# One 32-batch tanh recurrence between the two feed-forward passes of a first layer, in place of two 16-batch recurrences interleaved with them

## The chip, the core and the metric

The kernel runs on one NeuronCore of a Trainium2 chip. The core has a matrix engine (TensorE, "PE" in the profile, with its weight loads as "PEld"), a vector engine (VectorE, "DVE"), an activation engine (ScalarE, "ACT"), a general engine (GpSimd, "POOL") and a queue engine (SyncE, "SP") that issues DMAs. Each works through its own list of instructions in order and waits on semaphores for the others.

The metric is the device time of one execution in microseconds (us), the median of several runs.

## What is computed

The model has two layers. The first one is, with x of shape (32 batches, 256 times, 128 features):

```
x = x + mamba(layernorm(x))        # both directions
x = x + ffn(layernorm(x))          # feed-forward with 8 experts
x = x + recurrence(layernorm(x))   # the change is here
x = x + ffn(layernorm(x))          # the same feed-forward again
```

The recurrence is a plain tanh network over time:

```
def recurrence(x, A, B, C, gamma, beta):
    xb = einsum('bsd,ed->sbe', x, B)
    def step(h, xb_t):
        h = tanh(h @ A.T + xb_t)
        return h, h @ C.T
    _, ys = scan(step, zeros(batch, d), xb)     # 256 steps
    out = transpose(ys, (1, 0, 2)) + x
    return layernorm(out) * gamma + beta
```

A step needs the state of the step before it, so the 256 steps of a batch can only follow each other; batches are independent. A second layer (two attentions and two feed-forwards with routed experts) comes behind and is not touched.

## The kernel before

All activations stay in on-chip memory as 16 chunks `xs[c]` of 128 features by 512 columns, a chunk being two batches of 256 times. The first layer after the mamba part is `first_layer` (L894). It runs two passes over the 16 chunks:

- `before(c)`: the feed-forward `l0_ffn` (L693), then `enter`, which normalises the chunk and writes it into `xin`, the input of the recurrence.
- `behind(c)`: `leave`, which multiplies the states with C (`rnnC`, L856), adds `xin`, normalises (L863) and adds to `xs[c]`; then `l0_ffn` again.

`l0_ffn` is a generator of 23 pieces: norm (L326 to L330, with `spread`, L311 to L320), a short convolution (L715), the router (L724 to L764), eight experts (L770 to L781, a product, a SiLU, four transposed broadcasts of the weights, a multiplication), an output product (L785), a second norm, a down projection with GELU (L796, L798) and an up projection whose sum into `x` (L803) is the last thing a chunk does. Each call also has SP issue two of 60 DMAs that fill a table in HBM with zeros (L673). `enter` and `leave` add 4 and 5 pieces.

`pipeline` (L336) weaves the chunks: a new one starts every five rounds, and in each round every active chunk emits its next piece. So some five to six chunks are in work at a time. What this order gives is what each engine runs; a scheduler in the framework may still swap neighbouring instructions that do not depend on each other.

The recurrence is held by `Recurrence` (L818), here in two groups of 16 batches (chunks 0 to 7 and 8 to 15). `chain` (L831) emits one step per call. For every 32 steps a product with B (`rnnB`, L837, 512 columns that lie 1 KB apart in `xin`) fills one bank of PSUM; each step then adds the product of A with the last state to its 16 columns of that bank (`rnnA`, L846) and takes tanh into `hs` (L849). In the profile an L846 or L837 product in fp32 is two matmuls and two weight loads.

`Beside` (L867) places the steps: each piece that a pipeline emits earns one step, which the active groups take in turn. Chain 0 begins when chunks 0 to 7 have entered, chain 1 when 8 to 15 have. After the first pipeline L920 runs chain 0 to its end, and as long as both are active their steps alternate; the rest of chain 1 goes beside the second pipeline, until chunk 8 leaves, which first runs chain 1 to its end (L915).

The first layer's PSUM has eight banks: six for the tag `m`, one for each chain.

Of the kernel before, what the change touches and what calls it, by code (L numbers as in the profile page):

```python
# [13 lines left out]
F32 = mybir.dt.float32  # L14
# [8 lines left out]
P = 128  # L23
B, L = 32, 256
NT = B * L
CH = 512
NCH = NT // CH
# [247 lines left out]
def hybrid_kernel(ctx: ExitStack, tc, x_d, out_d, d, packs):  # L275
# [18 lines left out]
    def W(name):  # L294
        return com.view(late_t["com"], name) if name in com.at else att.view(late_t["att"], name)
# [7 lines left out]
    def two(ap):  # L303
        return ap.rearrange("p (b t) -> p b t", b=2)
# [18 lines left out]
    def norm(pool, ps, src, bufs):  # L323

        cps = ps.tile([P, CH], F32, tag="m", name="cps")
        nc.tensor.matmul(cps, K("center"), src, start=True, stop=True)  # L326
        sq = pool.tile([P, CH], F32, tag="ln_sq", name="sq", bufs=bufs)
        nc.scalar.activation(sq, cps, AF.Square)
        xc = pool.tile([P, CH], F32, tag="ln_xc", name="xc", bufs=bufs)
        nc.scalar.copy(xc, cps)  # L330
        yield
        rb = yield from spread(pool, ps, sq, 1e-5)
        return xc, rb


    def pipeline(make, every, count=NCH, beside=None, newest=False):  # L336

        active, c, n = [], 0, 0
        while c < count or active:
            if c < count and n % every == 0:  # L340
                active.append(make(c))
                c += 1
            n += 1
            for g in active[::-1] if newest else list(active):
                if next(g, "end") == "end":
                    active.remove(g)
                if beside:
                    beside()

# [1 line left out]
    with ExitStack() as ph:  # L353
# [8 lines left out]
        with tc.tile_pool(name="mtap", bufs=1) as tp, tc.tile_pool(name="mprep", bufs=2, space=PSUM) as pp:  # L362
            tap_t = tp.tile([P, tap.n], F32, name="tap_t")
            nc.scalar.dma_start(tap_t, d["tap"].partition_broadcast(P))
            for k, s in enumerate("fb"):

                wconv[s] = wp.tile([P, DCONV, DI], F32, name="wconv" + s)
                at, _, w = tap.at[s]
# [20 lines left out]
        p2 = ph.enter_context(tc.tile_pool(name="m2", bufs=2))  # L389
        ps = ph.enter_context(tc.tile_pool(name="mps", bufs=2, space=PSUM))  # L390
# [23 lines left out]
        def unit(k):  # L414
# [225 lines left out]
            if s == "b":  # L640
# [4 lines left out]
                yield  # L645

        pipeline(unit, 16, 2 * NCH)

    late = ctx.enter_context(tc.tile_pool(name="late", bufs=1))
# [15 lines left out]
    n = SPARE // 30  # L665
# [141 lines left out]
    def padded(pool, n):  # L807
        out = [pool.tile([P, 2, L + 2], F32, name=f"xp{k}") for k in range(n)]
        for t in out:
            nc.gpsimd.memset(t[:, :, 0:2], 0.0)  # L810
        return out

    NG = 2
    GB, GC = B // NG, NCH // NG

    class Recurrence:  # L818
        def __init__(self, pool, g):
            self.g = g  # L820
            self.xin = pool.tile([P, GB, L], F32, name=f"xin{g}")
            self.hs = pool.tile([P, L, GB], F32, name=f"hs{g}")

        def enter(self, c, pool, ps):

            at = 2 * (c % GC)
            xc, rb = yield from norm(pool, ps, xs[c], 2)
            nc.vector.tensor_mul(self.xin[:, at : at + 2, :], two(xc), two(rb))
            yield

        def chain(self, ps):  # L831
            n = CH // GB
            for t in range(L):
                j = t % n
                if j == 0:
                    hps = ps.tile([P, n, GB], F32, tag=f"h{self.g}", name="hps", bufs=1)
                    nc.tensor.matmul(  # L837
                        hps,
                        W("rnnB"),
                        self.xin[:, :, t : t + n].rearrange("p b t -> p t b"),  # L840
                        start=True,
                        stop=False,
                        skip_group_check=True,
                    )
                if t:
                    nc.tensor.matmul(  # L846
                        hps[:, j, :], W("rnnA"), self.hs[:, t - 1, :], start=False, stop=True, skip_group_check=True
                    )
                nc.scalar.activation(self.hs[:, t, :], hps[:, j, :], AF.Tanh)  # L849
                yield  # L850

        def leave(self, c, pool, ps):

            at = 2 * (c % GC)
            yps = ps.tile([P, CH], F32, tag="m", name="yps")
            nc.tensor.matmul(  # L856
                yps, W("rnnC"), self.hs[:, :, at : at + 2].rearrange("p t b -> p b t"), start=True, stop=True
            )
            o = pool.tile([P, CH], F32, tag="ro", name="o", bufs=2)
            nc.vector.tensor_add(two(o), two(yps), self.xin[:, at : at + 2, :])  # L860
            yield
            xc, rb = yield from norm(pool, ps, o, 2)
            nc.vector.scalar_tensor_tensor(o, xc, W("rnn_g"), rb, ALU.mult, ALU.mult)  # L863
            nc.vector.scalar_tensor_tensor(xs[c], o, W("rnn_b"), xs[c], ALU.add, ALU.add)
            yield

    class Beside:  # L867


        def __init__(self, rate):  # L870
            self.rate, self.due, self.chains = rate, 0.0, []

        def begin(self, chain):
            self.chains.append(chain)

        def step(self):
            chain = self.chains.pop(0)
            if next(chain, "end") != "end":
                self.chains.append(chain)
                return True  # L880
            return False

        def __call__(self):
            self.due = min(self.due + self.rate, 2.0)
            while self.chains and self.due >= 1.0:
                self.due -= 1.0
                self.step()

        def end(self, chain):

            while chain in self.chains:
                self.step()

    def first_layer():  # L894
        with ExitStack() as ph:
            p1 = ph.enter_context(tc.tile_pool(name="l1", bufs=1))
            p2 = ph.enter_context(tc.tile_pool(name="l2", bufs=2))
            ps = ph.enter_context(tc.tile_pool(name="lps", bufs=6, space=PSUM))
            pads = padded(p1, 4)
            groups = [Recurrence(p1, g) for g in range(NG)]  # L900
            beside = Beside(1.0)
            chains = [g.chain(ps) for g in groups]
            done = set()

            def before(c):
                g = c // GC
                yield from l0_ffn(c, p2, ps, pads)
                yield from groups[g].enter(c, p2, ps)
                done.add(c)
                if done >= set(range(g * GC, (g + 1) * GC)):  # L910
                    beside.begin(chains[g])

            def behind(c):
                if c == GC:
                    beside.end(chains[1])  # L915
                yield from groups[c // GC].leave(c, p2, ps)
                yield from l0_ffn(c, p2, ps, pads)

            pipeline(before, 5, NCH, beside)
            beside.end(chains[0])  # L920
            pipeline(behind, 5, NCH, beside)

# [696 lines left out]
    def l1_attn_b(fetch, send):  # L1621
        with ExitStack() as ph:
# [45 lines left out]
            pipeline(chunk, 16, newest=True)  # L1668

    first_layer()  # L1670
    early.close()
    send0, blocks0, fetch0 = l1_ffn(0)
# [5 lines left out]
    with tc.tile_pool(name="last", bufs=4) as p, tc.tile_pool(name="lastps", bufs=2, space=PSUM) as ps:  # L1678

        def leave(c):  # L1680
            yield from fetch1(c, p, ps, 3)
            nc.sync.dma_start(out_d[:, c * CH : (c + 1) * CH], xs[c])

        pipeline(leave, 1)
# [31 lines left out]
```

## Time and profile before

| | us |
|---|---|
| median of 3 runs | 6238.78 (6236.38 to 6243.42) |
| profiled execution | 6234.39 |
| its span | 6232.7 |
| mamba part ends (L644, last) | 2059.3 |
| first norm product of `first_layer` (L326) | 2068.3 |
| first rnnB product (L837) | 2321.6 |
| last xin written (L828, starts) | 2493.95 |
| first rnnC product (L856) | 2640.5 |
| last tanh (L849, starts) | 2857.4 |
| last feed-forward ends (L803, starts) | 3118.7 |

The whole span by engine, and in 40 equal slices of 155.8 us:

```profile
PE 5356.8 (86%) x25850; PEld 2792.6 (45%) x25922; DVE 4117.2 (66%) x7006; ACT 2710.2 (43%) x4424; POOL 3289.4 (53%) x3074
...
PE   6777777777777799999998888897998999997997
PEld 2222222222221466965544444445884444443886
DVE  5998999989989554044555555655665666665565
...
PEclk9888988888988899598989999998998999998998
```

In the first row stands the busy time of each engine, its share of the span and its number of instructions. In the others each digit is one slice: the busy share in tenths, or, in the row PEclk, the clock that TensorE was granted, in tenths of full speed. The first layer after the mamba part covers the slices 14 to 20. The 17th slice (2493 to 2649 us) stands out: PE busy, weight loads at nine tenths, DVE at zero and the clock at five tenths. The recurrence as a whole, in both chains:

```profile
L846 PE MATMUL hps<-hs,com_t x1020: 178/374/396, 2326.3 to 2857.0; 128*128 128x16 f32 x170
L849 ACT ACTIVATE hs<-hps x512: 157/184/203, 2323.6 to 2857.4; 128x16 f32<-128x16 f32 x171
...
L837 PE MATMUL hps<-xin,com_t x32: 1021/1043/1224, 2321.6 to 2828.8; 128*128 128x512 f32 x32
```

The three numbers behind the colon are the shortest, median and longest time of one instruction in ns, then come the first and last start in us. 510 products with A (of two matmuls each), 512 tanh and 16 products with B lie between 2321 and 2858 us.

### The profile page before, as it was taken

The page shows a single profiled execution, that of the slowest core. Times are in us where ns is not written, and L with a number is a line of the kernel's source. Part 1 is how long each engine was busy: PE and PEld are TensorE (multiplying, and loading weights), DVE is VectorE, ACT ScalarE, POOL GpSimd, SP SyncE. Part 2 cuts the span into 40 slices and gives each one's busy share as a digit, 9 for nine tenths or more (in the row PEclk, how much of TensorE's full clock was granted, in tenths as well). Part 3 has the DMA queues.
Part 4 walks back from the last instruction along what each step waited for, and adds up shares of the span by engine and source line. Part 5 has one row for each costly group of instructions (what it writes and reads, how often), then busy time and mean ns, then how long its engine had stood idle before and what let it go on. Part 6 is the DMA issues. An engine that isn't in the chain of part 4 may idle for free. (4 is left out here: it accounts for less than half of the span.)

```text
span 6232.7 us, 73938 instructions
## 1 busy us (share of the span) xinstructions
PE 5356.8 (86%) x25850; PEld 2792.6 (45%) x25922; DVE 4117.2 (66%) x7006; ACT 2710.2 (43%) x4424; POOL 3289.4 (53%) x3074
## 2 busy tenths in 40 slices
PE   6777777777777799999998888897998999997997
PEld 2222222222221466965544444445884444443886
DVE  5998999989989554044555555655665666665565
ACT  4665666666655354344434444342221333333221
POOL 5888888888888564044634444443332333333332
PEclk9888988888988899598989999998998999998998
DMA  3333333333332740000000000004550000000555
GB/s 148 123 123 116 123 116 123 116 123 116 126 112 109 304 185 1 1 1 1 1 1 10 9 8 8 11 8 129 186 172 19 20 16 18 18 11 12 188 188 189
DMA packets 190421, 512.13 MB, mean 82 GB/s; under 512 B 22177, under 2 KB 75169, under 8 KB 164961
## 3 DMA queue, kind: packets, MB, share of 16 engines
q1 hardware_dynamic: 172192, 468.00, 21.1%
q0 software_dynamic: 17280, 35.69, 1.7%
q8 instruction: 205, 3.36, 0.2%
q10 hardware_dynamic: 576, 3.71, 0.2%
q14 instruction: 168, 1.37, 0.1%
HBM read 359.93 MB, written 147.38 MB: 81 GB/s over the span
## 5 line engine op out<-in xcount | busy, mean ns | idle before, releaser
L612 POOL TENSOR_TENSOR dBu<-widedu,bcB 128x512 f32<-128x512 f32 x1024 | 1294.8, 1284 | 249.9 <-DVE h L621 162.0
L621 DVE TENSOR_TENSOR_SCAN h<-dA,dBu 128x512 f32<-128x512 f32 x768 | 942.5, 1227 | 119.8 <-ACT dA L608 30.4
L574 PE MATMUL yps<-pr,cst_t 128*32 128x512 f32 x2048 | 579.9, 645 | 244.8 <-POOL pr L569 102.7
L936 POOL TENSOR_SCALAR_AFFINE_SELECT e<-e 128x2048 f32<-128x2048 f32 (+1 forms) x256 | 343.3, 1353 | 597.2 <-ACT e L1047 386.1
L1412 POOL DMA_INDIRECT rows_out<-y,goes x284 | 271.8, 957 | 559.9 <-DVE y L1410 464.2
L1000 DVE TENSOR_REDUCE nm<-st 128x2 f32<-128x512 f32 x512 | 324.3, 684 | 268.5 <-PE st L996 267.4
L608 ACT ACTIVATE dA<-widedelta,Af 128x510 f32<-128x510 f32 x512 | 348.5, 688 | 300.9 <-DVE h L621 222.0
L608 ACT ACTIVATE dA<-widedelta,Ab 128x510 f32<-128x510 f32 x512 | 345.0, 686 | 272.7 <-DVE h L621 209.5
L1187 ACT ACTIVATE s<-s 128x512 f32<-128x512 f32 x284 | 179.0, 630 | 578.3 <-DVE s L1186 309.2
L574 PEld LDWEIGHTS yps<-pr,cst_t 128*32 128x32 f32 x2048 | 86.8, 112 | 704.8 <-POOL pr L569 228.0
L315 POOL TENSOR_TENSOR rstd<-var,cst_t 128x4 f32<-128x4 f32 x128 | 130.0, 1016 | 516.2 <-DVE var L313 514.4
L781 POOL TENSOR_TENSOR comb<-comb,ye 128x512 f32<-128x512 f32 x224 | 284.8, 1275 | 182.0 <-DVE ye L780 75.2
L1060 ACT ACTIVATE e<-st 128x512 f32<-128x512 f32 x512 | 272.0, 598 | 184.5 <-PE st L1056 154.8
L569 POOL TENSOR_TENSOR pr<-hs,bcC 128x512 f32<-128x512 f32 x256 | 334.4, 1306 | 13.7 <-DVE hs L621 13.7
L621 DVE TENSOR_TENSOR_SCAN hs<-dA,dBu 128x512 f32<-128x512 f32 x256 | 308.3, 1204 | 48.8 <-ACT dA L608 47.3
L1301 POOL DMA_INDIRECT rows_in<-xt,slot x256 | 253.6, 991 | 119.0 <-issue 98.7
L623 DVE TENSOR_TENSOR pr<-h,bcC 128x1024 f32<-128x1024 f32 x256 | 309.8, 1210 | 8.5 <-PE yps L574 0.5
L1188 DVE TENSOR_TENSOR hh<-s,u_ps 128x512 f32<-128x512 f32 x284 | 195.4, 688 | 172.0 <-ACT s L1187 168.0
L1393 PE MATMUL g_ps<-xb,gu 128*128 128x256 f32 x1136 | 302.6, 389 | 3.6 <-ACT xb L1376 2.3
L1402 PE MATMUL yps<-dn,hh 128*128 128x128 f32 x2272 | 291.5, 276 | 5.9 <-DVE hh L1188 5.8
L1393 PE MATMUL u_ps<-xb,gu 128*128 128x256 f32 x1136 | 293.3, 381 | 0.0
L1402 PEld LDWEIGHTS yps<-dn,hh 128*128 128x128 f32 x2272 | 282.8, 192 | 15.3 <-DVE hh L1188 7.8
(353 smaller groups left out, 11248.5 us busy)
## 6 DMA issues: line engine op xcount, KB each, us to landing
gu<-in_gu SPq DMA_DIRECT2D x142, 512.0 KB, 3.7
rows_in<-zero SPq DMA_DIRECT2D x60, 1170.0 KB, 18.7
widedelta<-delta_d SPq DMA_DIRECT2D x64, 1024.0 KB, 5.5
widedu<-du_d SPq DMA_DIRECT2D x64, 1024.0 KB, 5.1
dn<-in_dn SPq DMA_DIRECT2D x142, 256.0 KB, 3.9
bcB<-xdbl_d SPq DMA_DIRECT2D x32, 1024.0 KB, 5.0
bcC<-xdbl_d SPq DMA_DIRECT2D x32, 1024.0 KB, 6.9
xr<-rows_in SPq DMA_DIRECT2D x142, 130.0 KB, 3.8
```

What stands on the lines that cost most here:

```text
L569: nc.gpsimd.tensor_mul(pr, hs, bc["C"][:, g, :])
L574: nc.tensor.matmul(yps[32 * k : 32 * k + 32, :], K("states"), pr, start=False, stop=(g == 3), skip_group_check=True, tile_position=(0, 32 ...
L608: nc.scalar.activation(two(dA)[:, :, 1:L], two(steps)[:, :, 1:L], AF.Exp, scale=A[s][:, at : at + 1])
L612: nc.gpsimd.tensor_mul(dBu, duw[:, k, :], bc["B"][:, g, :])
L621: scan[0] = nc.vector.tensor_tensor_scan(*views, 0.0, ALU.mult, ALU.add)
L623: nc.vector.tensor_mul(pr2, h2, bc["C"][:, g, :].unsqueeze(1).to_broadcast([P, 2, CH]))
L781: nc.gpsimd.tensor_add(comb, comb, ye)
L936: nc.gpsimd.affine_select(e, e, [[0, n], [sign, P]], ALU.is_gt, 0.0, base=base, channel_multiplier=-sign)
L1000: nc.vector.tensor_reduce(n1[:, x, 2 * r : 2 * r + 2], o.rearrange("p (j k) -> p j k", j=2), AX.X, ALU.max, negate=True,)
L1060: nc.scalar.activation(e0[:, r], o.rearrange("p (j k) -> p j k", j=2), AF.Exp)
L1393: nc.tensor.matmul(o[:, j, :], gu[:, at : at + P], xb, start=True, stop=True)
L1402: nc.tensor.matmul(yps[:, t, :], hh[:, k, t * P : (t + 1) * P], dn[:, k, :], start=(k == 0), stop=(k == FF // P - 1),)
```

## The change

One chain carries all 32 batches. `xin` and `hs` are one tile each, a step works on 32 columns, a bank of PSUM holds 16 steps instead of 32, and the chain has two banks under one tag. `Beside` is gone, and with it the call in `pipeline`: the first pipeline runs to its end, then all 256 steps are emitted, then the second pipeline.

```diff
-    def pipeline(make, every, count=NCH, beside=None, newest=False):
+    def pipeline(make, every, count=NCH, newest=False):
...
                 if next(g, "end") == "end":
                     active.remove(g)
-                if beside:
-                    beside()
...
-    NG = 2
-    GB, GC = B // NG, NCH // NG
     class Recurrence:
-        def __init__(self, pool, g):
-            self.g = g
-            self.xin = pool.tile([P, GB, L], F32, name=f"xin{g}")
-            self.hs = pool.tile([P, L, GB], F32, name=f"hs{g}")
+        def __init__(self, pool):
+            self.xin = pool.tile([P, B, L], F32, name="xin")
+            self.hs = pool.tile([P, L, B], F32, name="hs")
         def enter(self, c, pool, ps):
-            at = 2 * (c % GC)
+            at = 2 * c
...
         def chain(self, ps):
-            n = CH // GB
+            n = CH // B
             for t in range(L):
                 j = t % n
                 if j == 0:
-                    hps = ps.tile([P, n, GB], F32, tag=f"h{self.g}", name="hps", bufs=1)
+                    hps = ps.tile([P, n, B], F32, tag="h", name="hps", bufs=2)
...
         def leave(self, c, pool, ps):
-            at = 2 * (c % GC)
+            at = 2 * c
...
-    class Beside:
...
             pads = padded(p1, 4)
-            groups = [Recurrence(p1, g) for g in range(NG)]
-            beside = Beside(1.0)
-            chains = [g.chain(ps) for g in groups]
-            done = set()
+            recurrence = Recurrence(p1)
             def before(c):
-                g = c // GC
                 yield from l0_ffn(c, p2, ps, pads)
-                yield from groups[g].enter(c, p2, ps)
-                done.add(c)
-                if done >= set(range(g * GC, (g + 1) * GC)):
-                    beside.begin(chains[g])
+                yield from recurrence.enter(c, p2, ps)
             def behind(c):
-                if c == GC:
-                    beside.end(chains[1])
-                yield from groups[c // GC].leave(c, p2, ps)
+                yield from recurrence.leave(c, p2, ps)
                 yield from l0_ffn(c, p2, ps, pads)
-            pipeline(before, 5, NCH, beside)
-            beside.end(chains[0])
-            pipeline(behind, 5, NCH, beside)
+            pipeline(before, 5)
+            for _ in recurrence.chain(ps):
+                pass
+            pipeline(behind, 5)
```

More of the change, by code (lines that the diff above doesn't have):

```diff
@@ L865, in leave @@
             yield
-    class Beside:
[L870 to L892, printed above, removed]
     def first_layer():
```

## The prediction

> **What bounds the kernel now.** The page's chain of waits holds only the last 6% of the span, so it says nothing of this change, which lies between about 2060 and 3120 us. I read that stage by windows: first the busy time of every engine, then the tanh row alone, then the instructions in order of time at the few places that price a step.
>
> Busy time by stretch (stretch, its length, busy us and instructions of each engine, granted TensorE clock, DMA share, GB/s):
>
> ```profile
> core 0: us, PE busy (x) PEld busy (x) DVE busy (x) ACT busy (x) POOL busy (x), PEclk, DMA share, GB/s
> 2100.00:2320.00 220.00, 219.08 (x1039) 132.03 (x1039) 133.15 (x337) 114.70 (x172) 139.57 (x117) 1.00 0.72 277
> ...
> 2496.00:2640.00 144.00, 143.97 (x604) 134.11 (x603) 0.00 (x0) 53.94 (x294) 0.00 (x0) 0.50 0.00 1
> ...
> 2830.00:2857.00 27.00, 18.54 (x63) 15.22 (x62) 0.00 (x0) 5.70 (x31) 0.00 (x0) 0.50 0.00 1
> 2866.00:3038.00 172.00, 172.00 (x771) 97.36 (x772) 100.49 (x248) 85.41 (x127) 102.96 (x84) 1.00 0.00 1
> ```
>
> The two feed-forward pipelines keep PE full at clock 1.00. Two stretches hold nothing but the chain: 144 us with both chains and 27 us with one, both at clock 0.50. The tanh row, cut where the stage changes:
>
> ```profile
> 2320.00:2494.60 174.60, 18.76 (x105) 0.93 0.00 1
> 2494.60:2640.50 145.90, 54.46 (x296) 0.50 0.00 1
> 2640.50:2746.30 105.80, 5.18 (x28) 0.84 0.00 1
> 2746.30:2827.70 81.40, 9.16 (x51) 0.98 0.00 1
> 2827.70:2858.00 30.30, 5.89 (x32) 0.50 0.00 1
> ```
>
> Of 512 steps, 184 (105 + 28 + 51) run beside feed-forwards, 328 in the open, 296 of those in pairs. The end of each feed-forward (L803), one per chunk, gives the pace:
>
> ```profile
> 2141.05 0.75 DVE L803 SCALAR_TENSOR_TENSOR x<-m,com_t,x 128x512 f32<-128x512 f32 x1 [0.96 <-PE m L802]
> 2300.16 0.75 DVE L803 SCALAR_TENSOR_TENSOR x<-m,com_t,x 128x512 f32<-128x512 f32 x1 [0.96 <-PE m L802]
> ...
> 2746.29 0.75 DVE L803 SCALAR_TENSOR_TENSOR x<-m,com_t,x 128x512 f32<-128x512 f32 x1 [2.05 <-PE m L802]
> 2866.10 0.75 DVE L803 SCALAR_TENSOR_TENSOR x<-m,com_t,x 128x512 f32<-128x512 f32 x1 [1.92 <-PE m L802]
> 3037.93 0.75 DVE L803 SCALAR_TENSOR_TENSOR x<-m,com_t,x 128x512 f32<-128x512 f32 x1 [1.92 <-PE m L802]
> 3118.70 0.75 DVE L803 SCALAR_TENSOR_TENSOR x<-m,com_t,x 128x512 f32<-128x512 f32 x1 [4.97 <-PE m L802]
> ```
>
> Chunks 0 to 7 without a chain: (2300.16 - 2141.05) / 7 = 22.73 us each. Second pipeline, chunks 3 to 10, no chain left: (3037.93 - 2866.10) / 7 = 24.55 us; its last five chunks drain in 80.8 us.
>
> Last, one chain alone in order of time (start, us, engine, line), at half and at full clock:
>
> ```profile
> 2838.03 0.18 ACT L849 ACTIVATE hs<-hps 128x16 f32<-128x16 f32 x1 [0.70 <-PE hps L846]
> 2838.27 0.50 PEld L846 LDWEIGHTS hps<-hs,com_t 128*128 128x128 f32 x2 [0.38 <-ACT hs L849]
> 2838.27 0.61 PE L846 MATMUL hps<-hs,com_t 128*128 128x16 f32 x2 [0.27 <-ACT hs L849]
> 2838.91 0.18 ACT L849 ACTIVATE hs<-hps 128x16 f32<-128x16 f32 x1 [0.70 <-PE hps L846]
> ...
> 2485.18 0.18 ACT L849 ACTIVATE hs<-hps 128x16 f32<-128x16 f32 x1 [0.48 <-PE hps L846]
> 2485.84 0.18 ACT L849 ACTIVATE hs<-hps 128x16 f32<-128x16 f32 x1 [0.48 <-PE hps L846]
> ```
>
> A lone step is 0.88 us at clock 0.50 (2838.91 - 2838.03) and 0.66 at full clock. Two chains that alternate also need 0.88 us a pair (42 tanh in 20 us, less the rnnB products), since each keeps PE busy while the other is in tanh.
>
> **The change, part by part.** In the built order of the changed kernel all 256 tanh stand together on ACT, with PE's chain between the last product of the first pipeline and the first rnnC product. On PE, POOL and SP everything else stands in the old order, with the same counts; on DVE some small routing operations swap places. So three stretches change.
>
> *First pipeline, without 105 steps beside it.* Chunk 11 ends at 2141.05 + 11 x 22.73 = 2391.1. For the drain I take the second pipeline's, 80.8, less five times the difference of the paces (24.55 - 22.73): 71.7. The last xin (L828) is then written at 2462.8; before it was at 2493.95. **Saved: 31 us**, 0.30 per step moved. In the saturated part a step cost about 0.21 (pace 26.1 with 16 steps against 22.73); 0.21 for all would make 22 us, the low end.
>
> *The chain, alone.* 255 rnnA products replace 510, each on 32 columns. No row has 32 columns, so bound the step. Below: 0.88, if width is free; nothing can make it less at this clock, as weight load, product and tanh wait for each other. PE: a 128x512 product takes 1.03 us a pass at half clock (first norm of the stage, L326: 2.07 for two), 2.0 ns a column, so 16 more columns add 0.032 us a pass; the first pass can lie beside the second weight load (0.29 + 0.22 us), the second can't. ACT: 0.18 us for 16 columns against 0.60 for 512 (L328) is 0.8 ns a column: 0.013. I take 0.88 + 0.032 + 0.013 = 0.925; with both passes and a hand-over somewhat slower, 1.0 at the top. 255 x 0.925 = 236 us.
>
> The rnnB products are still 16, of 512 strided columns, 1.04 us a pass (L837), 2.08 each, the same at either clock. The second bank changes little: in the built order two stand ahead of step 1 (4.2 us), the other 14 each behind the first rnnA of a bank, while PE would wait for one tanh (0.27 us idle in the row above). At 2827.75 a rnnB product in a lone chain started, and the next tanh came at 2830.11, 2.36 us later, against 0.93 for a plain step: 1.43 extra, 14 times, 20 us; with the wait for PE's own last product (new with the change) up to 2.0. Two banks save only the tanh that before stood ahead of the product. Behind each waiting product PE holds the rest of the chain and then the whole second pipeline; none of that could start anyhow, since a chunk's rnnC product takes its two batches at all 256 times and so needs the last tanh. Chain: 4.2 + 0.2 + 236 + 20 = 260, say **262 us**, against 2640.5 - 2493.95 = 146.6 before: **115 more**. Bounds: 248 and 288.
>
> *Second pipeline, without 79 steps beside it and 32 in its midst.* From the first rnnC product (2640.5) to chunk 0's L803 it took 105.8 us, with 28 steps in it, mostly at half clock. The first pipeline needed 72.8 us (2068.3 to 2141.05) for its first chunk; with about 11 for the leave ahead of it and up to 22 for the other chunks' leaves (4.6 of them at some 4.8 us of PE) that makes 84 to 106. By the steps' price (28 x 0.4) it is 95, the middle; I take 95: 11 saved. Chunk 0 to 3 took 119.8 us; at 24.55 it is 73.6: 46 saved, 29 of them the lone end of chain 1 that chunk 8 forced (L915). **Saved: 57 us.** From chunk 3 on nothing changes.
>
> Cost nothing: the 60 zero-fill DMAs of the feed-forwards, which SP issues in the same order and which end near 2255 us, before any chain; the wider stride of states for rnnC, as its rows (64 bytes apart, 1.03 us) equal those of rnnB (1 KB apart, 1.04).
>
> **Sum:** -31 + 115 - 57 = +27 us. The profiled execution took 6234.4 (span 6232.7), so 6261.7. The median before is 4.4 above that execution; I forecast **6264**.
>
> **A rule against the row.** The Trainium skill, "TensorE: Matmul & The Clock Gate", under "HAM oscillation", wants no idle gap on PE over some 3.4 us for the clock to stay full. The lone chain has gaps of 0.27 us, so by the rule it runs at 0.66 + 0.03 = 0.69 a step: 255 x 0.69 + 4.4 + 14 x 1.6 = 203 us, and the change gains 32 us. The rows say 0.50 for the lone chain and even for two chains with PE busy 143.97 of 144 us: short gaps do not suffice here. I go by the rows.
>
> **Rivals.**
> - *Cheaper by both ends* (0.13): width free (0.88 a step: 248 us) and chunk 0 of the second pipeline at 84: +27 - 14 - 11 = +2, 6241 on the median, no change to be told. For: a tanh is mostly fixed cost. Against: PE streams columns at a fixed rate in every row.
> - *Full clock* (0.06): the single chain keeps the gate open: -32, about 6207, faster. Against: every lone step after the first few us of such a stretch is at 0.50.
> - *Dearer steps* (0.15): 1.0 a step and 2.0 per rnnB product: 255 + 28 + 5 = 288, +53, 6291. Decided by the step over 0.98.
> - *Chain still beside the feed-forwards*: excluded by the built order.
> - My forecast, 0.66, its own range 6247 to 6282.
>
> About 0.2% (12.5 us) is what a measurement of this kernel tells from no change: faster than 6226 has 0.06 (the clock), within it 0.14, slower 0.80. Range 6238 to 6291.
>
> **What would show it.** Right: tanh to tanh 0.91 to 0.95 at clock 0.50, some 260 us with DVE and POOL empty, L803 of chunks 0 to 11 at 22.7 us throughout, last L828 near 2463. Wrong: clock 1.00 inside the chain; a step at 0.88 or at 1.0; a first pipeline that drains no faster without the chain, which would make the loss 31 us larger.

## The result and the profile after

| | us |
|---|---|
| median after (5 runs) | 6275.6 (6269.23 to 6276.02) |
| median before (5 runs beside them) | 6243.42 (6236.38 to 6251.6) |
| ratio, 95% interval | 1.0047 (1.0033 to 1.0061), i.e. some 29 us (21 to 38) |
| profiled execution after, its span | 6275.6, 6273.9 |

The change makes the kernel 0.5% slower, close to the forecast of 6264. Below, "the stage" is the first layer behind the mamba part, from its first norm product to its last feed-forward end. First the kernel before, by windows over all engines, cut where the stage changes: first pipeline, open stretch of the chains, second pipeline to the end of chunk 0's feed-forward, and the rest of it (stretch, length, busy us and instructions of each engine, granted clock, DMA share, GB/s).

```profile
2068.30:2493.90 425.60, 414.85 (x1944) 255.91 (x1944) 216.15 (x546) 204.64 (x390) 228.22 (x192) 0.95 0.45 172
2493.90:2640.50 146.60, 146.02 (x611) 135.95 (x611) 0.69 (x1) 54.65 (x297) 0.00 (x0) 0.50 0.00 1
2640.50:2746.30 105.80, 98.78 (x402) 61.34 (x403) 45.83 (x120) 37.85 (x83) 37.78 (x32) 0.84 0.00 1
2746.30:3119.40 373.10, 355.81 (x1586) 210.26 (x1585) 188.41 (x457) 170.99 (x315) 196.26 (x162) 0.93 0.00 1
```

The same four stretches of the kernel after, in the same view:

```profile
2078.40:2471.40 393.00, 379.43 (x1728) 225.43 (x1728) 215.45 (x546) 192.61 (x286) 228.06 (x192) 0.96 0.49 186
2471.40:2726.10 254.70, 184.95 (x542) 135.47 (x542) 0.69 (x1) 50.61 (x256) 0.00 (x0) 0.51 0.00 0
2726.10:2823.60 97.50, 88.55 (x345) 49.73 (x346) 45.58 (x120) 33.64 (x55) 37.80 (x32) 0.85 0.00 1
2823.60:3150.70 327.10, 319.67 (x1416) 179.78 (x1415) 189.30 (x457) 158.75 (x231) 196.04 (x162) 0.98 0.00 1
```

Line against line: -32.6, +108.1, -8.3 and -46.0. The stage is 21 us longer. DVE and POOL do the same work in the pipelines as before; what left them is PE and ACT work of the chain. In the second line all engines but PE and ACT stand still for 255 us, and PE has only half its clock.

A step of the chain in order of time, after (in this kernel L831 is the product with B, L840 the product with A, L843 the tanh):

```profile
2560.41 0.20 ACT L843 ACTIVATE hs<-hps 128x32 f32<-128x32 f32 x1 [0.72 <-PE hps L840]
2560.66 0.50 PEld L840 LDWEIGHTS hps<-hs,com_t 128*128 128x128 f32 x2 [0.42 <-ACT hs L843]
2560.66 0.63 PE L840 MATMUL hps<-hs,com_t 128*128 128x32 f32 x2 [0.29 <-ACT hs L843]
2561.33 0.20 ACT L843 ACTIVATE hs<-hps 128x32 f32<-128x32 f32 x1 [0.72 <-PE hps L840]
...
2600.33 2.05 PE L831 MATMUL hps<-xin,com_t 128*128 128x512 f32 x2
2600.56 0.20 ACT L843 ACTIVATE hs<-hps 128x32 f32<-128x32 f32 x1 [0.72 <-PE hps L840]
...
2602.69 0.20 ACT L843 ACTIVATE hs<-hps 128x32 f32<-128x32 f32 x1 [1.94 <-PE hps L840]
```

Tanh to tanh is 0.92 us (2561.33 - 2560.41). With a rnnB product (L831) in between it is 2.13 (2602.69 - 2600.56). Twice the columns cost 0.02 us of product (0.63 against the 0.61 of the lone chain before) and 0.02 of tanh (0.20 against 0.18).

Outside the stage the two profiled executions differ by 20 us more: 10 in the mamba part ahead of it and 10 behind it, where the instructions are the same. Three of the runs below take that up.

### The profile page after: what moved, and what is told of

Read it like the earlier page. It is cut to its first block, busy times and chain, and to the rows that moved or that the text cites. A ratio compares the mean times of both kernels' runs of the same rounds, so it can differ in the third digit from the quotient of the medians.

```text
span 6273.9 us, 72769 instructions
## 1 busy us (share of the span) xinstructions
PE 5339.4 (85%) x25412; PEld 2722.0 (43%) x25412; DVE 4123.3 (66%) x7006; ACT 2677.1 (43%) x4168; POOL 3289.1 (52%) x3074
```

## The experiments

The runs come in three groups, each on one chip with runs of the kernel before beside them. Their times compare within a group only. In the first (`again`, `two_between`, `first_only`, `fill512`) the kernel before took 6238.48 us, in the second (`fill256`, `one_bank`, `joined`, `joined_plain`) 6291.13, in the third (`before_again`, `after_again`) 6273.1 in a single run. Line numbers in the views are those of each run's own kernel.

### The changed kernel again

> The changed kernel once more. The first layer's stage (first norm product to last feed-forward end) was 21 us longer than before in the two profiles, the whole span 41, the medians 32. If the 20 us outside the stage (10 in the mamba part ahead of it, 8 in the expert blocks behind) are scatter between executions, this median lies 15 to 30 us over before's, and the mamba part in this and the other profiles of this series moves by about 10 us with no relation to the change. If they belong to the change, the mamba part of this profile is again near 2069 us and that of every kernel that keeps two chains near 2059.

6278.98 us, ratio 1.0057 (1.0044 to 1.0071), so 27 to 44 us over before. The stage was 1073 us from the first norm product to the last L801, against 1071.5 in the first profile and 1050.4 before. The mamba part ended at 2070.6. By what was expected this speaks for the program: the median lies 40 us over before, and the two kernels of this group that keep two chains had their mamba part end at 2060.4 and 2060.2. The last pair of runs speaks against it.

### Two chains, both between the pipelines

```diff
-            pipeline(before, 5, NCH, beside)
-            beside.end(chains[0])
-            pipeline(behind, 5, NCH, beside)
+            pipeline(before, 5, NCH)
+            with tc.issue_after(spread_end[0].ins):
+                beside.end(chains[0])
+                beside.end(chains[1])
+            pipeline(behind, 5, NCH)
```

> Two chains of 16 batches as before, but both alternating between the two pipelines and nothing beside them. Theory (the loss is the overlap that was given up, merging costs nothing): pairs at 0.99 us all in, as in the open stretch of before (148 pairs in 146 us), so 256 pairs in 252 us against 255 for the single chain; total equal to the changed kernel within 5 us. Rival (a single chain is slow because nothing fills PE's wait for tanh, and two alternating chains would fill it): the 0.27 us gap per step comes back, some 60 us, total near 6215.

Here `spread_end[0]` is the last broadcast product of the first pipeline (the lines of `spread` that keep it are left out), so both chains stand behind it.

6265.21 us, ratio 1.0040 (1.0026 to 1.0054). The stage by windows (stretches and columns as above):

```profile
2069.50:2462.50 393.00, 379.55 (x1729) 225.93 (x1730) 215.49 (x546) 192.66 (x286) 227.84 (x192) 0.96 0.49 186
2462.50:2708.10 245.60, 244.42 (x1053) 224.06 (x1052) 0.69 (x1) 94.14 (x511) 0.00 (x0) 0.54 0.00 1
2708.10:2804.60 96.50, 87.59 (x346) 49.52 (x347) 45.57 (x120) 33.92 (x56) 37.79 (x32) 0.87 0.00 1
2804.60:3131.80 327.20, 319.73 (x1416) 179.80 (x1415) 189.47 (x457) 158.80 (x231) 195.81 (x162) 0.98 0.00 1
```

256 pairs take 246 us, the 256 merged steps 255. The rival's 60 us aren't there: two alternating chains do fill PE (244.42 of 245.60), but with twice the weight loads. The total is 14 us under the changed kernel's, though, and not equal to it within 5 as expected. The stage is 1062.3 us, 11 more than before and 10 less than after. So the stage's 21 us have two parts of about the same size: moving the chains out of the pipelines makes 11, and merging them 10, of which 9 are in the open stretch.

### Chain 0 beside the first pipeline, chain 1 all ahead of the second

```diff
             beside.end(chains[0])
-            pipeline(behind, 5, NCH, beside)
+            beside.end(chains[1])
+            pipeline(behind, 5, NCH)
```

and chunk 0's first piece of `leave` is put behind the last product of chain 1, so that the scheduler doesn't bring it forward.

> Two chains, chain 0 beside the first pipeline as before, but chain 1 run to its end ahead of the second pipeline. Theory: the first pipeline ends near 2494 us as before, the open stretch has about 150 pairs (149 us) and then some 105 lone steps of chain 1 at 0.88 us and three rnnB products (98 us), the second pipeline takes 97 + 326 us as in the changed kernel; total about 45 us over before, some 15 to 20 over the changed kernel. Rival (the overlap with the second pipeline brings nothing, since PE is full there): total equal to before within 10 us.

6293.6 us, ratio 1.0087 (1.0073 to 1.0102), so 45 to 64 us over before. Open stretch and second pipeline by windows:

```profile
2495.00:2744.00 249.00, 218.33 (x838) 193.16 (x838) 0.69 (x1) 74.99 (x407) 0.00 (x0) 0.50 0.00 0
2744.00:2843.70 99.70, 90.79 (x346) 51.59 (x347) 45.64 (x119) 33.93 (x56) 37.78 (x32) 0.83 0.00 1
2843.70:3170.70 327.00, 319.57 (x1416) 179.81 (x1416) 189.55 (x457) 158.91 (x231) 195.71 (x162) 0.98 0.00 1
```

The first pipeline took 425.6 us as before, the open stretch 249.0 (149 + 98 were expected), the second pipeline 100 us to its first chunk and 327 from there (97 and 326 were expected). The stage is 50 us longer than before: that is what it was worth to have 79 steps of chain 1 beside the second pipeline, though PE is nearly full there.

### A filler product behind each step

```diff
             for t in range(L):
...
-                    nc.tensor.matmul(
+                    step = nc.tensor.matmul(
                         hps[:, j, :], W("rnnA"), self.hs[:, t - 1, :], start=False, stop=True, ...
                     )
+                    with tc.issue_after(step.ins):
+                        nc.tensor.matmul(junk[:, 0:512], identb, mask_t[:, 0:512], start=True, stop=True)
```

> The changed kernel with one bf16 product of 512 columns, whose result nobody reads, behind each rnnA product, while PE waits for tanh. Theory (the clock follows how much PE streams, and a lone chain streams too little): clock 1.00 in the chain, 0.70 to 0.75 a step, chain some 205 us in place of 255, total about 6225. Rival (the clock in this stretch stays at 0.50 whatever stands in the gap): the filler at half clock takes 0.43 us and a weight load against a gap of 0.27, so about 1.2 us a step, chain some 320 us, total about 6340.

6238.32 us, ratio 0.9996 (0.9986 to 1.0005): the time of the kernel before, though not the 6225 that were expected. The stage alone is 1038.1 us, 34 less than after and 13 less than before, so here too some 10 us lie outside it. The chain, first as a whole, then two stretches within it:

```profile
2472.80:2692.50 219.70, 207.17 (x797) 107.31 (x797) 0.69 (x1) 50.61 (x256) 0.00 (x0) 0.80 0.00 1
```

```profile
2485.00:2507.00 22.00, 22.00 (x68) 12.71 (x68) 0.00 (x0) 4.15 (x21) 0.00 (x0) 0.50 0.00 0
2510.00:2537.00 27.00, 24.66 (x110) 11.95 (x109) 0.00 (x0) 6.91 (x35) 0.00 (x0) 1.00 0.00 1
```

In order of time, in a stretch at full clock and in one at half (L841 is the product with A, L845 the filler, L846 the tanh):

```profile
2560.11 0.20 ACT L846 ACTIVATE hs<-hps 128x32 f32<-128x32 f32 x1 [1.88 <-PE hps L841]
2560.36 0.30 PEld L841 LDWEIGHTS hps<-hs,com_t 128*128 128x128 f32 x2 [0.38 <-ACT hs L846]
2560.36 0.41 PE L841 MATMUL hps<-hs,com_t 128*128 128x32 f32 x2
...
2560.61 0.38 PE L845 MATMUL junk<-mask_t 128*128 128x512 bf16 x1
2560.81 0.20 ACT L846 ACTIVATE hs<-hps 128x32 f32<-128x32 f32 x1 [0.50 <-PE hps L841]
...
2601.35 0.61 PE L845 MATMUL junk<-mask_t 128*128 128x512 bf16 x1
2601.58 0.20 ACT L846 ACTIVATE hs<-hps 128x32 f32<-128x32 f32 x1 [0.73 <-PE hps L841]
...
2602.50 0.20 ACT L846 ACTIVATE hs<-hps 128x32 f32<-128x32 f32 x1 [0.72 <-PE hps L841]
```

0.70 us a step at full clock, 0.92 at half, as without the filler: on a plain step it costs nothing in either (only a step with a rnnB product at half clock took up to 2.40 us from tanh to tanh in place of 2.13), and it raises the mean clock to 0.80. Expected was 1.00 throughout and 205 us; it was 219.7, since the clock changed fourteen times within the chain, in stretches of 7 to 31 us. The rival's 1.2 us a step is refuted.

### Half the filler

The same with 256 columns.

> As fill512, but 256 columns per filler. Theory (the clock is granted window by window according to how much PE streams in it, and 512 columns per step lie near the limit, since the clock there went to and fro): fewer windows at full clock, mean clock 0.50 to 0.60 in the chain, chain 240 to 255 us, total 0 to 15 us under the changed kernel. Rival (any product in the gap counts, whatever its width): clock and time as with 512.

6318.99 us, ratio 1.0042 (1.0030 to 1.0055), about that of the changed kernel in the other groups.

```profile
2473.70:2728.90 255.20, 235.74 (x797) 142.70 (x797) 0.69 (x1) 50.61 (x256) 0.00 (x0) 0.51 0.00 1
```

The clock stays at 0.51 and the chain at 255 us, at the upper end of what was expected. So not any product in the gap opens the clock: 256 columns a step are too few, and 512, where it went to and fro, seem to be near the limit. PE busy 235.74 of 255.20, next to 207.17 of 219.70 with 512, shows again that the busy row doesn't tell it.

### One bank of PSUM

```diff
-                    hps = ps.tile([P, n, B], F32, tag="h", name="hps", bufs=2)
+                    hps = ps.tile([P, n, B], F32, tag="h", name="hps", bufs=1)
```

> The changed kernel with one bank of PSUM for the chain in place of two. Theory: the second bank only lets a rnnB product start while a tanh runs, so without it each of 15 bank changes costs some 0.3 to 0.5 us more (2.6 us from tanh to tanh, as in the lone chain of before, against 2.13), chain 260 to 263 us in place of 255, total 5 to 8 us over the changed kernel. Rival (the second bank hides most of a product): 1.5 us and more per change, over 20 us. As a second single-chain kernel with another layout it also shows whether the mamba part is again near 2070 us.

The chain took 263.3 us in place of 254.7. A change of bank in order of time:

```profile
2482.28 0.20 ACT L843 ACTIVATE hs<-hps 128x32 f32<-128x32 f32 x1 [0.72 <-PE hps L840]
2482.53 2.07 PE L831 MATMUL hps<-xin,com_t 128*128 128x512 f32 x2 [0.29 <-ACT hs L843]
...
2484.90 0.20 ACT L843 ACTIVATE hs<-hps 128x32 f32<-128x32 f32 x1 [2.43 <-PE hps L840]
```

Tanh to tanh it takes 2.62 us (2484.90 - 2482.28) in place of 2.13, 15 times: the product now starts behind the tanh and waits for it (2482.53), where with two banks it started 0.23 ahead of it. So the second bank hides the tanh and not the product. The last 1 us is at the start, where the steps ran at half clock from the first on. The total, 6315.53 us and 1.0044 (1.0028 to 1.0060), can't tell so little. Its mamba part ended at 2063.5.

### Both groups joined in one step, with and without the filler

Chain 0 runs 96 steps beside the first pipeline; then 160 steps multiply group 0 at time 96 + r and group 1 at time r together; the last 96 of chain 1 go beside the second pipeline. States of both groups lie in one tile, so that one access pattern takes both rows.

```diff
...
+        h = hs[:, LEAD : LEAD + 2 * BOTH, :].rearrange("p (g r) b -> p r g b", g=2)
...
+        for r in range(BOTH):                            # LEAD = 96, BOTH = 160
+            j = r % n                                    # n = 16 steps a bank
+            if j == 0:
+                hps = ps.tile([P, n, 2, GB], F32, tag="h", name="hps", bufs=2)
+                for g, at in enumerate((LEAD + r, r)):
+                    groups[g].fed(hps[:, :, g, :], at, n)    # rnnB
...
+            step = nc.tensor.matmul(into, W("rnnA"), last, start=False, stop=True, skip_group_check=True)
+            with tc.issue_after(step.ins):
+                nc.tensor.matmul(junk, identb, mask_t[:, 0:CH], start=True, stop=True)
+            nc.scalar.activation(h[:, r, :, :], hps[:, j, :, :], AF.Tanh)
...
             beside.end(chains[0])
+            together(groups, hs, ps)
+            beside.begin(chains[1])
             pipeline(behind, 5, NCH, beside)
```

> Both ideas: chain 0 runs its first 96 steps beside the first pipeline, then 160 steps carry both groups in one product (group 0 at step 96 + r, group 1 at step r) with the 512-column filler, then the last 96 steps of chain 1 go beside the second pipeline. Theory (overlap keeps its worth of 0.3 us a step, and a 32-column step costs 0.70 at full clock, as fill512 has shown): first pipeline ends near 2491 us, joined stretch 125 to 140 us against 147 for the open stretch of before, lone end of chain 1 some 15 us shorter; total 20 to 35 us under before. Rival (products in two halves and tanh over two strided blocks cost what the clock gains): equal to before within 10 us.

> The same without the filler. Theory: the joined stretch at half clock, 160 x 0.93 + 9 x 1.4 = 161 us against 147 for pairs of before, lone end 15 us shorter: total equal to before within 10 us, so that the difference to the run with the filler, 25 to 35 us, is the clock's alone.

With the filler: 6229.96 us against 6291.13, ratio 0.9907 (0.9886 to 0.9928), faster than the kernel before. Without it: 6262.71, ratio 0.9963 (0.9947 to 0.9979). With the filler, the joined stretch, the second pipeline to the end of chunk 0, and from there to the end of chunk 3; then the joined stretch without it:

```profile
2488.60:2617.10 128.50, 117.64 (x508) 64.97 (x518) 0.69 (x1) 31.64 (x160) 0.00 (x0) 0.90 0.00 1
2617.10:2736.70 119.60, 112.86 (x487) 72.51 (x488) 45.16 (x120) 42.68 (x124) 37.97 (x32) 0.84 0.00 1
2736.70:2817.70 81.00, 81.00 (x385) 48.85 (x385) 42.84 (x108) 39.70 (x82) 44.40 (x36) 0.98 0.00 1
```

```profile
2494.00:2650.10 156.10, 114.65 (x358) 90.60 (x358) 0.69 (x1) 31.52 (x160) 0.00 (x0) 0.50 0.00 0
```

128.5 and 156.1 us are about what was expected (125 to 140, and 161): the clock is worth 28 us here. Both totals are better than the best that was expected, by some 25 and 15 us. The stages are 49 and 23 us shorter than before, within what the ratios give (45 to 72 and 13 to 33 us), and the profile shows where the surplus lies: to the end of chunk 0 the second pipeline took 120 and 119 us against 105.8, as more steps stand there, but from there to the end of chunk 3 it took 81 us with the filler and 79 without, where before took 119.8. Chain 1 has only 96 steps left there, in place of 111, and nearly all go beside the chunks, so the open end that chunk 8 forced is gone as a whole and not by half.

### Before and after once more, for the part outside the stage

> The kernel before, profiled a second time, for the 20 us outside the first layer's stage (10 of them in the mamba part). If the mamba part's time is scatter of the clock windows, it lies anywhere from 2058 to 2072 us here; if it belongs to the program, it is again 2059 to 2060, as in the three kernels with two chains of 16.

> The changed kernel, profiled a third time, beside the kernel before on the same chip. If it belongs to the program, the mamba part is again 2069 to 2071 us, some 10 us over that of the kernel before; if it is scatter, anywhere from 2058 to 2072. The first layer's stage differs by 21 us as in the first pair of profiles either way.

Single runs: 6288.41 us for the kernel before, whose other run on this chip took 6273.1, and 6312.18 for the changed one. The kernel before, mamba part as a window, in its first profile:

```profile
0.00:2059.30 2059.30, 1528.21 (x4008) 443.33 (x4008) 1809.72 (x1733) 1232.21 (x1554) 1728.95 (x1357) 0.88 0.31 119
```

and in the second:

```profile
0.00:2070.60 2070.60, 1535.13 (x4008) 446.26 (x4008) 1811.50 (x1733) 1231.70 (x1554) 1726.05 (x1357) 0.87 0.31 118
```

The same kernel, the same 4008 products, 11 us apart: DVE and ACT are busy for about the same time, PE for 7 us more, at a lower mean clock. So the 10 us in the mamba part are within what one program shows in two executions, though perhaps on different chips; that the clock is the cause is argued from these rows, not shown by a run. In this pair, both on one chip, the two kernels' mamba parts ended at 2070.6 and 2069.7, within 1 us of each other. The stage, in contrast, was 1049.8 us in this second profile of before and 1071.4 in the third of after: 21.6 apart, as in the first pair. The whole spans, 6286.7 and 6310.4, are 23.7 apart, so here nearly all of the loss lies within the stage.

## Why the prediction was right

| step of the prediction | foreseen | measured |
|---|---|---|
| first pipeline shorter | 31 us | 32.6 |
| a step on 32 columns | 0.925 us | 0.92 |
| its granted clock | 0.50 | 0.51 |
| extra for a rnnB product | 1.43 us | 1.21 |
| chain in all | 262 us | 254.7 |
| second pipeline to chunk 0 | 95 us | 97.5 |
| from chunk 0 to chunk 3 | 73.6 us | 73.6 |
| the stage | +27 us | +21 (three profiles of after against two of before: 21 to 23) |
| the total | +25 | +29 by the ratio (21 to 38) |

The mechanism was as put: 184 of the 512 narrow steps, which ran beside the pipelines at about 0.30 us each (32.6 us for the 105 of the first), now stand in the open, where a merged step takes 0.92 us at half clock, hardly less than a pair did. `two_between` shows that the place of the chain alone makes about half of the loss, `first_only` what the overlap with the second pipeline is worth; the other half is the merging, since a merged step takes 0.92 us where an alternating pair took 0.88, and the two-chain stretch also had a little more clock (0.54 against 0.51).

The stage came out 6 us shorter than the sum, and the term that was mis-sized is the chain, 7 us too long. 3 of them are in the rnnB products (14 x 0.22). The row of the old trace was read rightly, 2.36 us from the start of the product to the next tanh, and it is the same after (2602.69 - 2600.33); but with two banks the product starts 0.23 us ahead of the tanh that ends the step before (2600.33 and 2600.56), and the prediction counted the 2.36 as if it started with it. 2 more are in the two products at the start, of which the second already runs beside the first tanh (2473.20 to 2474.28 in the trace), 1 in four steps at full clock before it fell, and the rest in my rounding up from 260.

The second pipeline to chunk 0 was priced at 0.4 us a step because its 28 steps were taken to run mostly at half clock. The row of that stretch has a mean clock of 0.84, and only 11 of the steps lie in its 20 us at half (2640.5 to 2660.4); measured, it gained 8.3 us and not 11.

That the total comes so near is in part luck. The forecast stood 2 us under its own sum (6234.4 + 27 + 4.4 = 6266), the stage fell 6 us short of it, and what made up for both lies outside the stage, which the prediction took as unchanged. In the first pair of profiles the rest of the kernel is 20 us longer, and by the ratios the totals of the first comparison and of `again` lie 8 and 13 us above what the stage gives. `two_between`, with two chains and a mamba part of 2060.4 us, lies 14 us above its stage as well. In the other groups nothing of the kind is seen: `fill256` and `one_bank` lie 26 and 28 us over before with stages 21 and 34 us longer, and in the last pair 23.7 us of span stand against 21.6 of the stage. All five profiles of a single chain with two banks had their mamba part at 2069 to 2071, while those of the kernels with two groups, `before_again` aside, had 2059 to 2065. Whether the changed program falls into the longer pattern more often than the old one stays open.

The rivals: full clock in the chain did not come by itself (0.51); the cheap ends did not meet (0.92, 97.5); the dear ones neither. The idle-gap rule (the Trainium skill, "TensorE: Matmul & The Clock Gate", "HAM oscillation"), which the prediction set aside for the rows, would by its estimate have made the change a gain of 32 us: PE's gaps in the chain were 0.29 us and its clock was half all the same.

## What to carry to other kernels

A serial chain is cheapest where other engines and PE have independent work: price each step twice, beside the work (here about 0.30 us for 16 columns) and alone (0.88, or 0.92 for 32), before moving it; a wider step that shortens the chain in count need not shorten it in time, if two narrow chains already alternated. Where a chain must stand alone, look at the granted clock rather than at PE busy: a product that nobody reads, put into the wait of each step, can pay for itself. And two chains at different places of time can share a step, as here, where their states lie in one tile.

## What the runs showed of the hardware

- The granted clock did not go with PE busy. Two chains kept PE busy 146.02 of 146.60 us, and weight loads 135.95, at clock 0.50; fillers of 256 columns a step, 235.74 of 255.20, at 0.51; fillers of 512 columns, 207.17 of 219.70, at 0.80, and 117.64 of 128.50 at 0.90 in the joined kernel. The two fillers differ in nothing but their columns, so how much PE streams does count. What exactly is counted, and where the limit lies, no run shows: with 512 columns the same steps ran at 0.50 for 22 us with PE busy throughout, and at 1.00 for 27.
- Half the clock doesn't double a step: 0.92 against 0.70 us, as only the weight loads (0.50 against 0.30 for the two) and the products stretch, and tanh and the hand-overs don't.
- A rnnB product with operands 1 KB apart takes 1.03 to 1.06 us a pass at the median, at either clock (L837 before, L832 in `fill512`), where a contiguous one of the same size takes 0.59 at full clock and 2.07 for two passes at half (L326 before).
- The same program's mamba part took 2059.3 and 2070.6 us in two executions, of different groups of runs; in the rows the clock (0.88 and 0.87) and with it PE's busy time (1528.21 and 1535.13 us) are what differs.
